# Spikes of a chunk in two batch rows instead of one block, mixed with the routing choices, and additions of returned rows in turns between two tiles

## The chip, the cores and the metric

The kernel runs on one core of a Trainium2 chip. The metric is the device time of one execution in microseconds (us). The engines of the core are TensorE (PE, with its weight loads as PEld), VectorE (DVE), ScalarE (ACT), GpSimd (POOL) and SyncE (SP), which here only issues DMAs. Each engine has its own queue and works through it in order; semaphores make one engine wait for another, or for its own earlier result.

## The reference, cut to what matters

The input `x` has 16 batch rows of 256 tokens with 256 channels; `cond` has one row of 256 channels for each batch row.

```python
# spikes: along the 256 tokens of a batch row
rates = relu(x) * 0.001
c = cond[:, None, :] + cumsum(rates, axis=1)
fl = floor(c)
prev = concatenate([floor(cond)[:, None, :], fl[:, :-1, :]], axis=1)
x = x + (fl - prev) / 0.001

# experts: 4096 tokens, 8 experts, 2 chosen for each token
shared = silu(xf @ w1) * (xf @ w3) @ w2
s = sigmoid(concatenate([xf, tf], -1) @ router_W)      # tf: cond of the token's batch row
topk_idx = top_k(s + router_bias, 2)
gates = s at the two, divided by their sum
routed = sum over the two chosen e of gate * (gelu(xf @ W1e[e]) @ W2e[e])
x = x + (shared + routed) / 3
```

## The kernel before

The 4096 tokens are cut into eight chunks of 512 tokens (two batch rows, `NB` = 2) and each chunk into four tiles of 128 tokens (`J` = 4). Channels lie on the partitions in two halves (`KD` = 2), so a chunk's spike data are 128 partitions by 2 x 2 x 256 elements.

**Spikes of one chunk** (`class Spikes`, driven by the generator `elementwise`). TensorE transposes the tokens (`turn`, L275), ScalarE writes `rates` (ReLU, L282) and a copy `xt` (L291). Then VectorE and ScalarE work on tags `tb`, `tot`, `base`, `ta`, `tc` of the pool `tmp`, one buffer each:
- `scan` (L306): a running sum in segments of 16 tokens, into `tb`; `keep` is zero at each segment's start.
- `sums` (L316, L320, L321): the segments' totals are copied shifted into `tot`, summed by a second scan into `base`, and added to every element, into `ta`.
- `start` and `whole` (ACT, L334, L343): `cond` is added as a bias, four times 256 elements, and the sum is cast to an integer in `tc`.
- `floor` (L358, L359): a compare and a subtract make the floor, in `tb` again, with the floor of `cond` in its first column (L348, VectorE).
- `spikes` (L370) and `add` (L378): the difference of neighbours, times 1000, plus `xt`, gives `x1`, for each batch row by itself.

From chunk 1 on, all but the last two take the whole chunk in one instruction of 1024 elements. Chunk 0 goes in three parts: two channel halves of its first batch row, then its second batch row.

**Routing of one chunk** (`route`). TensorE makes the logits `pl` (L426) from `x1`, VectorE clips them (`lt`, L435), TensorE turns them back (`pn`, L438), ScalarE takes the exponential (`ex`, L442), VectorE makes the sigmoid and picks the best expert twice (`first_best`, L452 to L458: maximum, compare, order, maximum, compare). These are instructions of 32 elements, each of which reads what the one before it wrote. `hot` (L470) marks both choices. From `hot` TensorE counts places (`pr`, L475 to L480) and turns `x1` into token rows (`px`, L496), which ScalarE copies into `x1t` (L497). VectorE makes the target rows `at_i` (L502 to L509), and GpSimd scatters the token rows to the buffer `xs` in device memory by indirect DMAs (L513).

**The shared expert** is a generator of work units (`unit`): `ph` matmuls (L536) of `x1` with `w1` and `w3`, silu on ScalarE (`as`, L546), a product on VectorE (`hs`, L547), `pa` matmuls (L563), and on VectorE `pa / 3` added to `x1t` (L574). A unit is spread by hand between the steps of `route` and `elementwise`: `next(ro)`, `next(el)`, `next(nxt)` and `unit()` stand in a written order in the main loop, where `el` is the chunk after the one that is routed. Between the start and the last chunk a scheduler may still change the order that results on each engine; at the start and from the last chunk on, the written order of PE, ACT and DVE is kept.

**Blocks and end.** After routing, SP loads up to 71 blocks of 128 rows; each goes through two expert products (L859, L881) and is scattered to `ys`. The last two shared chunks are left for the end, where they share time with `combine`: for each pair of token tiles (16 pairs) the returned rows `yc` are fetched from `ys`, and VectorE adds gate times row to `x1t`, twice for each tile, L996. Of the second choice's addition one input is the result of the first:

```python
            for j in range(2):
                last = x1ts[i][:, 2 * h + j, :, :FQ]
                for q in range(TOPK):
                    y = yc[:, j, TOPK - 1 - q]
                    nc.vector.scalar_tensor_tensor(
                        y, y, gates[:, q, t : t + 1], last, ALU.mult, ALU.add
                    )
                    last = y
```

The `pa` tiles lie in two PSUM buffers, and the `ph` tiles in three: a matmul into one of them waits until VectorE or ScalarE has read what was there.

Of the kernel before, what the change touches and what calls it, by code (L numbers as in the profile page):

```python
# [31 lines left out]
P = 128  # L32
N = 512
SEG = 16
# [4 lines left out]
def kernel(  # L39
# [203 lines left out]
    class Spikes:  # L243
# [3 lines left out]

        def __init__(self, i):  # L250
            def tile(tag, dt=F32, last=T, pool=tmp):
                return pool.tile([P, NB, KD, last], dt, tag=tag, name=f"{tag}_{i}")

            self.i, self.tile, self.xn = i, tile, xns.pop(i)
            self.xt = prep.tile([P, KD, N], F32, tag="xt", name=f"xt_{i}")
            self.rates = tile("rates")

        @staticmethod
        def cut(t, part):

            b, bb, k, kk = part
            if bb - b == 1:
                return t[:, b, k:kk, :].rearrange("p k t -> p (k t)")
            return t[:, b:bb, k:kk, :].rearrange("p b k t -> p (b k t)")

        def turn(self, part):

# [27 lines left out]
                xns[self.i + 2] = load_x(self.i + 2)  # L295

        def scan_tiles(self):
            self.seg = self.tile("tb")
            self.tot, self.base = self.tile("tot", last=NSEG), self.tile("base", last=NSEG)
            self.cs, self.ri = self.tile("ta"), self.tile("tc", I32)  # L300
            nc.vector.memset(self.tot[:, :, :, 0:1], 0.0)

        def scan(self, part):

            seg = self.cut(self.seg, part)
            nc.vector.tensor_tensor_scan(  # L306
                seg, keep[:, : seg.shape[1]], self.cut(self.rates, part), 0.0, ALU.mult, ALU.add
            )

        def sums(self, part):  # L310

            seg, tot, base, cs = (
                self.cut(t, part) for t in (self.seg, self.tot, self.base, self.cs)
            )
            n = tot.shape[1]
            nc.vector.tensor_copy(  # L316
                tot.rearrange("p (g s) -> p g s", s=NSEG)[:, :, 1:],
                seg.rearrange("p (g s q) -> p g s q", s=NSEG, q=SEG)[:, :, : NSEG - 1, SEG - 1],
            )
            nc.vector.tensor_tensor_scan(base, keep[:, :n], tot, 0.0, ALU.mult, ALU.add)  # L320
            nc.vector.tensor_tensor(  # L321
                cs.rearrange("p (s q) -> p s q", q=SEG),
                seg.rearrange("p (s q) -> p s q", q=SEG),
                base[:, :, None].to_broadcast([P, n, SEG]),
                ALU.add,
            )

        def start(self, part):
# [13 lines left out]

            nc.scalar.copy(self.cut(self.ri, part), self.cut(self.cs, part))  # L343

        def floor_tiles(self, pool=tmp, tag="tb", eng=nc.vector):

            self.fl = self.tile(tag, last=W, pool=pool)
            eng.tensor_copy(  # L348
                self.fl[:, :, :, 0].rearrange("p b k -> p k b"), cond_fl[:, :, ts(self.i, NB)]
            )  # L350
            self.x1 = x1s[self.i] = keepp.tile(
                [P, KD, N], F32, tag="x1", name=f"x1_{self.i}", bufs=6
            )

        def floor(self, part):

            up, ri = self.cut(self.cs, part), self.cut(self.ri, part)
            nc.vector.tensor_tensor(up, ri, up, ALU.is_gt)  # L358
            nc.vector.tensor_tensor(  # L359
                self.cut(self.fl, part).rearrange("p (g t) -> p g t", t=W)[:, :, 1:],  # L360
                ri.rearrange("p (g t) -> p g t", t=T),
                up.rearrange("p (g t) -> p g t", t=T),
                ALU.subtract,
            )

# [15 lines left out]

    def elementwise(i, sp=None):

        if sp is None:
            sp = Spikes(i)
            for k in range(KD):
                half = (0, NB, k, k + 1)
                pt = sp.turn(half)
                sp.rate(half, pt)
                sp.keep_x(half, pt)  # L390
            sp.next_load()
            yield
        part = (0, NB, 0, KD)
        sp.scan_tiles()
        sp.scan(part)
        yield
        sp.sums(part)
        yield
        sp.start(part)
        sp.whole(part)  # L400
        yield
        sp.floor_tiles()
        sp.floor(part)
        yield
        sp.spikes(part)
        yield
        sp.add(part)
        yield


# [2 lines left out]
    def route(i):  # L413
# [35 lines left out]
        def first_best(sc, q, key_at):  # L449
# [13 lines left out]
        nc.gpsimd.tensor_copy(  # L463
            x1t[:, :, :, FQ + 1], key_first[:, :, None].to_broadcast([P, J, NQ])
        )
        sel2 = small("sel2")
        nc.vector.scalar_tensor_tensor(sel2, hots[0], -BIG, sel, ALU.mult, ALU.add)
        hots.append(first_best(sel2, 1, small("second", (P, J))))
# [32 lines left out]
        row = small("row")  # L501
        nc.vector.tensor_tensor(row, pr, region, ALU.add)  # L502
        mine = small("mine", (P, TOPK, J, E))
        at = small("at", (P, TOPK, J))
        for q in range(TOPK):
            nc.vector.tensor_tensor(mine[:, q], row, hots[q], ALU.mult)
        nc.vector.tensor_reduce(at, mine, AX.X, ALU.add)
        at_i = small("at_i", (P, TOPK, J), I32)
        placed[i] = nc.vector.tensor_copy(at_i, at)  # L509
        yield  # L510
        for j in range(J):
            for q in range(TOPK):
# [101 lines left out]
    with tc.manual_schedule(engines={PE, ACT, DVE}):  # L614
        sp = Spikes(0)
        halves = [(0, 1, k, k + 1) for k in range(KD)]
        row = (1, 2, 0, KD)
        pts = [sp.turn(part) for part in halves]
        for part, pt in zip(halves, pts):
            sp.rate(part, pt)  # L620
        turn_cond()
        for part, pt in zip(halves, pts):
            sp.keep_x(part, pt)
        sp.scan_tiles()
        for part in halves:
            sp.scan(part)
            sp.sums(part)
            sp.start(part)
            sp.whole(part)
        cond_floor()  # L630
        sp.floor_tiles(pool=hid, tag="ht", eng=nc.gpsimd)
        pt = sp.turn(row)
        sp.rate(row, pt)
        sp.keep_x(row, pt)
        sp.next_load()
        for part in halves:
            sp.floor(part)
# [24 lines left out]
        unit(0.5)  # L662
# [7 lines left out]
    next(ro)  # L670
    next(el)
    next(ro)
    unit(0.5)
    next(ro)
    next(ro)
    next(ro)
    next(ro)
    next(el)
    unit(0.5)
    next(el)  # L680
    next(el)
    next(nxt)
    load_experts(0)
# [1 line left out]
    for i in range(2, NCHUNK):  # L685
        ro = route(i - 1)
        nxt = elementwise(i + 1) if i + 1 < NCHUNK else iter(())
        next(ro)
        next(el, None)
        unit()  # L690
        next(ro)
        next(el, None)
        next(ro)
        next(el, None)
        next(ro)
        unit()
        next(ro)
        next(el, None)
        next(ro)
        next(nxt, None)  # L700
        unit(1 + (i > 3 and i % 3 != 2) + (i == NCHUNK - 1))
        next(ro)
        next(el, None)
        next(ro)
        next(el, None)
        if i <= E // 2:
            load_experts(i - 1)
        el = nxt
# [3 lines left out]
    ro = route(NCHUNK - 1)  # L712
    next(ro)
    unit(0.5)
    next(ro)
    next(ro)
    next(ro)
# [268 lines left out]
    def combine():  # L986
        for n in range(SLOTS):
            fetch(n)
        for n, (i, h) in enumerate(pairs):
            yc = ycs.pop(n)  # L990
            for j in range(2):
                t = i * J + 2 * h + j
                last = x1ts[i][:, 2 * h + j, :, :FQ]
                for q in range(TOPK):
                    y = yc[:, j, TOPK - 1 - q]
                    nc.vector.scalar_tensor_tensor(  # L996
                        y, y, gates[:, q, t : t + 1], last, ALU.mult, ALU.add
                    )
# [56 lines left out]
```

## Time and profile before

| | us |
|---|---|
| median of 3 runs (336.89 to 337.3) | 337.07 |
| the profiled execution | 337.38 |
| its span, first to last instruction | 335.7 |
| busy: PE / DVE / POOL / ACT | 317.2 / 231.5 / 165.6 / 137.9 |

The profile is of one execution. The span is what its rows cover; some 1.7 us of that execution lie outside it. A row of the timeline has the start from the span's start, the busy time, the engine, the line of the kernel, the operation, the tile written and the tiles read, the shape, how many instructions were merged, and in brackets the idle time before it and what ended it. The granted clock of TensorE was 1.000 in the mean. A busy time runs to the end of the write, so on VectorE the next instruction can start before the last has ended.

### The profile page before, as it was taken

The page shows a single profiled execution, that of the slowest core. Times are in us where ns is not written, and L with a number is a line of the kernel's source. Part 1 is how long each engine was busy: PE and PEld are TensorE (multiplying, and loading weights), DVE is VectorE, ACT ScalarE, POOL GpSimd, SP SyncE. Part 2 cuts the span into 40 slices and gives each one's busy share as a digit, 9 for nine tenths or more (in the row PEclk, how much of TensorE's full clock was granted, in tenths as well). Part 3 has the DMA queues.
Part 4 walks back from the last instruction along what each step waited for, and adds up shares of the span by engine and source line. Part 5 has one row for each costly group of instructions (what it writes and reads, how often), then busy time and mean ns, then how long its engine had stood idle before and what let it go on. Part 6 is the DMA issues. An engine that isn't in the chain of part 4 may idle for free. (4 is left out here: it accounts for less than half of the span.)

```text
span 335.7 us, 6544 instructions
## 1 busy us (share of the span) xinstructions
PE 317.2 (94%) x1674; PEld 233.9 (70%) x1674; DVE 231.5 (69%) x656; ACT 137.9 (41%) x287; POOL 165.6 (49%) x197
## 2 busy tenths in 40 slices
PE   3799998999989999999999999999999999999985
PEld 2587644547546745746699998999999998474574
DVE  4677979999999996652467655555546551299993
ACT  4547385644675372040244443444444434201100
POOL 7000274787478687662045555555555565123220
PEclk9999999999999999999999999999999999999999
DMA  6999533242222112354456665765666662499913
GB/s 174 255 217 215 146 114 98 88 136 100 79 81 99 65 64 86 109 194 102 73 109 149 155 149 142 165 140 126 156 150 151 157 146 80 164 364 408 397 70 125
DMA packets 62534, 50.34 MB, mean 150 GB/s; under 512 B 42607, under 2 KB 52864, under 8 KB 62497
## 3 DMA queue, kind: packets, MB, share of 16 engines
q1 hardware_dynamic: 42240, 26.19, 32.0%
q0 software_dynamic: 7456, 20.86, 17.0%
q10 hardware_dynamic: 12800, 2.88, 5.0%
q8 instruction: 14, 0.23, 0.3%
q14 instruction: 24, 0.19, 0.2%
HBM read 27.44 MB, written 22.84 MB: 150 GB/s over the span
## 5 line engine op out<-in xcount | busy, mean ns | idle before, releaser
L536 PE MATMUL ph<-x,w_sb 128*128 128x512 f32 (+1 forms) x288 | 119.3, 561 | 4.9 <-DVE x L378 4.2
L890 POOL DMA_INDIRECT ys<-yb,to x67 | 66.2, 988 | 67.0 <-ACT yb L889 56.4
L513 POOL DMA_INDIRECT xs<-x1t,at_i x64 | 78.8, 1232 | 38.8 <-ACT xt L291 18.7
L536 PEld LDWEIGHTS ph<-x,w_sb 128*128 128x128 f32 x288 | 54.2, 196 | 53.5 <-issue 42.0
L859 PEld LDWEIGHTS phe<-xbt,w1e 128*128 128x128 f32 x536 | 70.3, 191 | 4.7 <-ACT hbt L867 0.9
L859 PE MATMUL phe<-xbt,w1e 128*128 128x128 f32 x536 | 70.7, 275 | 0.7 <-DVE xbt L832 0.7
L881 PE MATMUL py<-we,hbt 128*128 x268 | 68.9, 380 | 0.2 <-ACT hbt L867 0.2
L827 DVE COPY w1e<-we 128x512 f32 x67 | 29.1, 435 | 45.3 <-PE phe L859 43.8
L563 PE MATMUL pa<-w_sb,hs 128*128 128x256 f32 x256 | 58.2, 381 | 1.4 <-DVE x1t L574 1.1
L563 PEld LDWEIGHTS pa<-w_sb,hs 128*128 128x128 f32 x256 | 48.0, 190 | 11.1 <-issue 2.8
L881 PEld LDWEIGHTS py<-we,hbt 128*128 128x128 f32 x268 | 45.9, 191 | 3.9 <-ACT hbt L867 0.4
L546 ACT ACTIVATE as<-ph 128x512 f32<-128x512 f32 (+1 forms) x36 | 19.9, 553 | 64.5 <-PE ph L536 51.8
L867 ACT ACTIVATE hbt<-phe 128x256 f32<-128x256 f32 x67 | 25.8, 384 | 45.6 <-PE phe L859 35.2
L547 DVE TENSOR_TENSOR hs<-as,ph 128x512 f32<-128x512 f32 (+1 forms) x36 | 22.4, 623 | 27.5 <-PE ph L536 20.8
L889 ACT COPY yb<-py 128x256 f32<-128x256 f32 x67 | 24.9, 372 | 22.7 <-PE py L881 22.2
L832 DVE STREAM_TRANSPOSE xbt<-xb 128x256 f32<-128x256 f32 x67 | 29.3, 437 | 0.0
L306 DVE TENSOR_TENSOR_SCAN tb<-keep,rates 128x1024 f32<-128x1024 f32 (+2 forms) x10 | 18.8, 1876 | 1.4 <-ACT rates L282 1.3
L497 ACT COPY x1t<-px 128x512 f32<-128x512 f32 x16 | 8.6, 592 | 25.1 <-PE px L496 25.1
L589 POOL DMA_DIRECT2D out_dram<-yc x8 | 5.8, 729 | 23.9 <-DVE yc L996 22.1
L334 ACT ACTIVATE ta<-ta,cond_t 128x256 f32<-128x256 f32 x32 | 14.1, 498 | 8.1 <-DVE ta L321 7.1
L463 POOL COPY x1t<-first 128x16 f32<-128x16 f32 x8 | 4.2, 519 | 23.1 <-DVE first L456 23.1
L574 DVE SCALAR_TENSOR_TENSOR x1t<-pa,x1t 128x512 f32<-128x512 f32 x14 | 9.6, 684 | 6.3 <-PE pa L563 6.3
(135 smaller groups left out, 268.2 us busy)
## 6 DMA issues: line engine op xcount, KB each, us to landing
xb<-xs SPq DMA_DIRECT2D x184, 33.0 KB
yc<-ys SPq DMA_DIRECT2D x8, 512.0 KB
we<-ys SPq DMA_DIRECT2D x8, 512.0 KB
xn<-in_x_dram SPq DMA_DIRECT2D x7, 512.0 KB
xb<-xs ACTq DMA_DIRECT2D x84, 33.0 KB
we<-in_L_cond_W1e_dram SPq DMA_DIRECT2D x8, 256.0 KB
we<-in_L_cond_W2e_dram SPq DMA_DIRECT2D x8, 256.0 KB
out_dram<-yc POOLq DMA_DIRECT2D x8, 256.0 KB, 4.3
```

What stands on the lines that cost most here:

```text
L513: nc.gpsimd.indirect_dma_start(out=xs_w[(i * J + j) * TOPK + q][:, :], out_offset=bass.IndirectOffsetOnAxis(ap=at_i[:, q, j : j + 1], axis=0),
L536: nc.tensor.matmul(ph, lhsT=w[:, k, ts(u, P)], rhs=x1[:, k, cols], start=(k == 0), stop=(k == KD - 1),)
L546: nc.scalar.activation(act, ps[0], AF.Silu)
L547: nc.vector.tensor_tensor(ht[:, u, cols], act, ps[1], ALU.mult)
L563: nc.tensor.matmul(pa[:, q, :], lhsT=ht[:, s, ts(n * h + q, P)], rhs=w2_sb[:, s, :], start=(s == 0), stop=(s == KS - 1),)
L827: nc.vector.tensor_copy(w, we[:, bass.ds(off, KD * HE)])
L832: nc.vector.transpose(xt.rearrange("p g k r -> p g (k r)"), block[b].pop("xb")[:, :, :FQ])
L859: nc.tensor.matmul(ph[:, m, :].rearrange("p (g r) -> p g r", r=Q), lhsT=w[:, k, ts(m, P)], rhs=xt[:, :, k, :], start=(k == 0), stop=(k == ...
L867: nc.scalar.activation(ht, ph, AF.Gelu)
L881: nc.tensor.matmul(py, lhsT=ht[:, k, :], rhs=we[:, bass.ds(off + KD * HE + k * D, D)], start=(k == 0), stop=(k == KH - 1),)
L889: nc.scalar.copy(yb, py)
L890: nc.gpsimd.indirect_dma_start(out=ys_w[b][:, :], out_offset=bass.IndirectOffsetOnAxis(ap=to[:, b : b + 1], axis=0), in_=yb, in_offset=Non ...
```

## The change

Four things are done. A chunk's spikes go through `scan`, `sums`, `start`, `whole`, `floor`, `spikes` and `add` in two parts, one for each batch row (`one`, `two`); the parts are mixed in the written order. The running sums are made in place: the scan writes `tb`, the second scan reads the segments' last elements directly, and its sums are added to all segments but the first of a row, in `tb` again; the floor goes to `ta`, its first column is copied by ScalarE (for chunk 0 by GpSimd). In `route` a `yield` is put between the first and the second choice, so that work of `elementwise` can stand there, and the place `at_i` is reduced straight into integers. In `combine` the two tiles of a pair take turns: the first choice of both, then the second choice of both.

```diff
         def scan_tiles(self):
-            self.seg = self.tile("tb")
-            self.tot, self.base = self.tile("tot", last=NSEG), self.tile("base", last=NSEG)
-            self.cs, self.ri = self.tile("ta"), self.tile("tc", I32)
-            nc.vector.memset(self.tot[:, :, :, 0:1], 0.0)
+            self.cs = self.tile("tb")
+            self.upto, self.ri = self.tile("tot", last=NSEG), self.tile("tc", I32)
...
         def sums(self, part):
-            n = tot.shape[1]
-            nc.vector.tensor_copy(
-                tot.rearrange("p (g s) -> p g s", s=NSEG)[:, :, 1:],
-                seg.rearrange("p (g s q) -> p g s q", s=NSEG, q=SEG)[:, :, : NSEG - 1, SEG - 1],
-            )
-            nc.vector.tensor_tensor_scan(base, keep[:, :n], tot, 0.0, ALU.mult, ALU.add)
+            upto = self.cut(self.upto, part)
+            n = upto.shape[1]
+            cs = self.cut(self.cs, part).rearrange("p (s q) -> p s q", q=SEG)
+            nc.vector.tensor_tensor_scan(
+                upto, keep[:, :n], cs[:, :, SEG - 1], 0.0, ALU.mult, ALU.add
+            )
+            cs = cs.rearrange("p (g s) q -> p g s q", s=NSEG)[:, :, 1:]
+            upto = upto.rearrange("p (g s) -> p g s", s=NSEG)[:, :, : NSEG - 1, None]
             nc.vector.tensor_tensor(
-                cs.rearrange("p (s q) -> p s q", q=SEG),
-                seg.rearrange("p (s q) -> p s q", q=SEG),
-                base[:, :, None].to_broadcast([P, n, SEG]),
-                ALU.add,
+                cs, cs, upto.to_broadcast([P, n // NSEG, NSEG - 1, SEG]), ALU.add
             )
...
-        def floor_tiles(self, pool=tmp, tag="tb", eng=nc.vector):
-            self.fl = self.tile(tag, last=W, pool=pool)
-            eng.tensor_copy(
-                self.fl[:, :, :, 0].rearrange("p b k -> p k b"), cond_fl[:, :, ts(self.i, NB)]
-            )
+        def floor_tiles(self, copy=nc.scalar.copy):
+            self.fl = self.tile("ta", last=W)
+            copy(self.fl[:, :, :, 0].rearrange("p b k -> p k b"), cond_fl[:, :, ts(self.i, NB)])
...
     def elementwise(i, sp=None):
+        one, two = [(b, b + 1, 0, KD) for b in range(NB)]
         if sp is None:
             sp = Spikes(i)
-            for k in range(KD):
-                half = (0, NB, k, k + 1)
-                pt = sp.turn(half)
-                sp.rate(half, pt)
-                sp.keep_x(half, pt)
+            for part in (one, two):
+                pt = sp.turn(part)
+                sp.rate(part, pt)
+                sp.keep_x(part, pt)
             sp.next_load()
             yield
-        part = (0, NB, 0, KD)
         sp.scan_tiles()
-        sp.scan(part)
-        yield
-        sp.sums(part)
-        yield
-        sp.start(part)
-        sp.whole(part)
-        yield
-        sp.floor_tiles()
-        sp.floor(part)
-        yield
-        sp.spikes(part)
-        yield
-        sp.add(part)
+        sp.scan(one)
+        yield
+        sp.sums(one)
+        sp.start(one)
+        sp.whole(one)
+        sp.scan(two)
+        yield
+        sp.sums(two)
+        sp.start(two)
+        sp.whole(two)
+        sp.floor_tiles()
+        yield
+        sp.floor(one)
+        yield
+        sp.spikes(one)
+        sp.add(one)
+        sp.floor(two)
+        yield
+        sp.spikes(two)
+        sp.add(two)
         yield
...
         nc.gpsimd.tensor_copy(
             x1t[:, :, :, FQ + 1], key_first[:, :, None].to_broadcast([P, J, NQ])
         )
+        yield
         sel2 = small("sel2")
...
-        at = small("at", (P, TOPK, J))
-        nc.vector.tensor_reduce(at, mine, AX.X, ALU.add)
         at_i = small("at_i", (P, TOPK, J), I32)
-        placed[i] = nc.vector.tensor_copy(at_i, at)
+        with nc.allow_low_precision(reason="one whole number and zeros are added"):
+            placed[i] = nc.vector.tensor_reduce(at_i, mine, AX.X, ALU.add)
...
-        sp.floor_tiles(pool=hid, tag="ht", eng=nc.gpsimd)
+        sp.floor_tiles(copy=nc.gpsimd.tensor_copy)
...
     next(ro)
     next(el)
     next(ro)
+    next(el)
+    next(ro)
     unit(0.5)
     next(ro)
-    next(ro)
-    next(ro)
-    next(ro)
     next(el)
+    next(ro)
+    next(ro)
+    next(ro)
     unit(0.5)
-    next(el)
     next(el)
     next(nxt)
...
         next(ro)
         next(el, None)
         next(ro)
+        next(el, None)
+        next(ro)
         unit()
         next(ro)
         next(el, None)
...
         unit(1 + (i > 3 and i % 3 != 2) + (i == NCHUNK - 1))
         next(ro)
-        next(el, None)
         next(ro)
         next(el, None)
...
-            for j in range(2):
-                t = i * J + 2 * h + j
-                last = x1ts[i][:, 2 * h + j, :, :FQ]
-                for q in range(TOPK):
+            last = [x1ts[i][:, 2 * h + j, :, :FQ] for j in range(2)]
+            for q in range(TOPK):
+                for j in range(2):
+                    t = i * J + 2 * h + j
                     y = yc[:, j, TOPK - 1 - q]
                     nc.vector.scalar_tensor_tensor(
-                        y, y, gates[:, q, t : t + 1], last, ALU.mult, ALU.add
+                        y, y, gates[:, q, t : t + 1], last[j], ALU.mult, ALU.add
                     )
-                    last = y
+                    last[j] = y
```

More of the change, by code (lines that the diff above doesn't have):

```diff
@@ L250, in __init__, with tile @@
         def __init__(self, i):
-            def tile(tag, dt=F32, last=T, pool=tmp):
-                return pool.tile([P, NB, KD, last], dt, tag=tag, name=f"{tag}_{i}")
+            def tile(tag, dt=F32, last=T):
+                return tmp.tile([P, NB, KD, last], dt, tag=tag, name=f"{tag}_{i}")
             self.i, self.tile, self.xn = i, tile, xns.pop(i)
@@ L259, in cut @@
         def cut(t, part):
[L261 to L264, printed above, removed]
+            b, _, k, kk = part
+            return t[:, b, k:kk, :].rearrange("p k t -> p (k t)")
         def turn(self, part):
@@ L297, in scan_tiles @@
         def scan_tiles(self):
-            self.seg = self.tile("tb")
-            self.tot, self.base = self.tile("tot", last=NSEG), self.tile("base", last=NSEG)
-            self.cs, self.ri = self.tile("ta"), self.tile("tc", I32)
-            nc.vector.memset(self.tot[:, :, :, 0:1], 0.0)
+            self.cs = self.tile("tb")
+            self.upto, self.ri = self.tile("tot", last=NSEG), self.tile("tc", I32)
         def scan(self, part):
-            seg = self.cut(self.seg, part)
+            cs = self.cut(self.cs, part)
             nc.vector.tensor_tensor_scan(
-                seg, keep[:, : seg.shape[1]], self.cut(self.rates, part), 0.0, ALU.mult, ALU.add
+                cs, keep[:, : cs.shape[1]], self.cut(self.rates, part), 0.0, ALU.mult, ALU.add
             )
         def sums(self, part):
-            seg, tot, base, cs = (
-                self.cut(t, part) for t in (self.seg, self.tot, self.base, self.cs)
-            )
-            n = tot.shape[1]
-            nc.vector.tensor_copy(
-                tot.rearrange("p (g s) -> p g s", s=NSEG)[:, :, 1:],
-                seg.rearrange("p (g s q) -> p g s q", s=NSEG, q=SEG)[:, :, : NSEG - 1, SEG - 1],
-            )
-            nc.vector.tensor_tensor_scan(base, keep[:, :n], tot, 0.0, ALU.mult, ALU.add)
+            upto = self.cut(self.upto, part)
[3 more added lines that the diff above has]
+                upto, keep[:, :n], cs[:, :, SEG - 1], 0.0, ALU.mult, ALU.add
+            )
+            cs = cs.rearrange("p (g s) q -> p g s q", s=NSEG)[:, :, 1:]
+            upto = upto.rearrange("p (g s) -> p g s", s=NSEG)[:, :, : NSEG - 1, None]
             nc.vector.tensor_tensor(
-                cs.rearrange("p (s q) -> p s q", q=SEG),
-                seg.rearrange("p (s q) -> p s q", q=SEG),
-                base[:, :, None].to_broadcast([P, n, SEG]),
-                ALU.add,
+                cs, cs, upto.to_broadcast([P, n // NSEG, NSEG - 1, SEG]), ALU.add
             )
@@ L359, in floor @@
             nc.vector.tensor_tensor(
-                self.cut(self.fl, part).rearrange("p (g t) -> p g t", t=W)[:, :, 1:],
-                ri.rearrange("p (g t) -> p g t", t=T),
-                up.rearrange("p (g t) -> p g t", t=T),
+                self.cut(self.fl, part).rearrange("p (k t) -> p k t", t=W)[:, :, 1:],
+                ri.rearrange("p (k t) -> p k t", t=T),
+                up.rearrange("p (k t) -> p k t", t=T),
                 ALU.subtract,
@@ L672 @@
     next(ro)
+    next(el)
+    next(ro)
     unit(0.5)
+    next(ro)
+    next(el)
     next(ro)
@@ L676 @@
     next(ro)
-    next(ro)
-    next(el)
     unit(0.5)
-    next(el)
     next(el)
```

## The prediction, made before the changed kernel was run

> **What bounds the kernel now.** I read the page first.
>
> ```profile
> PE 317.2 (94%) x1674; PEld 233.9 (70%) x1674; DVE 231.5 (69%) x656; ACT 137.9 (41%) x287; POOL 165.6 (49%) x197
> PE   3799998999989999999999999999999999999985
> DVE  4677979999999996652467655555546551299993
> ```
>
> TensorE is the bound over the whole span. VectorE is full in two stretches only, slices 5 to 15 (routing, to about 125 us) and the end from 293 us. The change lies in both. So I cut the first at the matmul `pr` (L475), which waits for `hot`, and asked for the busy time from each `pr` to the next.
>
> ```profile
> 35.13:52.36 17.23, 16.28 (x72) 8.54 (x72) 14.77 (x39) 10.22 (x17) 10.56 (x9) 1.00 0.36 122
> 52.36:65.73 13.37, 13.16 (x62) 6.63 (x62) 12.86 (x39) 9.17 (x17) 7.89 (x6) 1.00 0.29 93
> 65.73:84.22 18.49, 18.05 (x90) 11.63 (x89) 17.92 (x43) 9.15 (x16) 14.64 (x13) 1.00 0.34 117
> 84.22:94.99 10.77, 10.14 (x55) 5.36 (x55) 10.32 (x35) 8.23 (x15) 5.91 (x4) 1.00 0.28 86
> 94.99:113.21 18.22, 17.34 (x86) 11.24 (x86) 17.72 (x43) 8.34 (x15) 14.85 (x13) 1.00 0.23 83
> 113.21:123.98 10.77, 10.22 (x54) 5.35 (x55) 10.36 (x34) 8.23 (x15) 7.17 (x6) 1.00 0.18 64
> ```
>
> Columns: stretch, length, then busy PE, PEld, DVE, ACT, POOL. Both PE and DVE are nearly full. Matmul starts lie 0.429 us apart (128x512), 0.216 (128x256) and 0.109 (transposes); by these the six stretches hold 15.8, 12.4, 17.6, 9.8, 16.7 and 9.8 us of matmuls, 82.1 in 88.85. TensorE loses 6.8 us, and DVE sets the pace. Two timelines give the rest.
>
> ```profile
> 112.97 0.19 DVE L470 TENSOR_TENSOR hot<-chosen,chosen 128x32 bf16<-128x32 f32 x1
> 113.07 0.69 DVE L370 TENSOR_TENSOR x<-tb 128x512 f32<-128x512 f32 x1
> 114.98 0.62 ACT L282 ACTIVATE rates<-pt 128x512 f32<-128x512 f32 x1
> 116.61 2.29 DVE L306 TENSOR_TENSOR_SCAN tb<-keep,rates 128x1024 f32<-128x1024 f32 x1
> 117.67 1.28 ACT L546 ACT_TABLE_LOAD   x1
> 118.97 0.60 ACT L546 ACTIVATE as<-ph 128x512 f32<-128x512 f32 x1
> ```
> ```profile
> 300.13 0.47 DVE L996 SCALAR_TENSOR_TENSOR yc<-yc,gates,x1t 128x256 f32<-128x256 f32 x1
> 300.64 0.48 DVE L996 SCALAR_TENSOR_TENSOR yc<-yc,gates 128x256 f32<-128x256 f32 x1
> 301.04 0.48 DVE L996 SCALAR_TENSOR_TENSOR yc<-yc,gates,x1t 128x256 f32<-128x256 f32 x1
> 326.45 1.99 PE L563 MATMUL pa<-w_sb,hs 128*128 128x256 f32 x8 [1.15 <-DVE x1t L574]
> 328.74 3.72 PE L563 MATMUL pa<-w_sb,hs 128*128 128x256 f32 x16 [0.30 <-DVE we L574]
> ```
>
> First: the rates of the next chunk end 2.63 us after `hot` starts (`pr`, `px`, `pt` on PE, two copies and the ReLU on ACT lie between), and DVE has 3.6 us of adds to do before its scan needs them. Second: an addition that reads what the one before it wrote starts 0.51 us after it, an independent one 0.40. All DVE rows obey this: next start at the end plus 0.034 if dependent, minus 0.084 if not, so a dependent step costs 0.118 more.
>
> **The start.** Each half of chunk 0 loses the copy L316 (steps of 0.21) and adds 240 instead of 256 elements. The second half's add, the floors behind it and `x1` come 0.44 us earlier, and so the first L536 matmuls, which waited 3.75 and 0.50 us. From 11.9 to 15.7 us those matmuls step at 0.427, half rate; if that phase doesn't move with them, half the gain is lost. I take 0.35. The changed instruction list lets chunk 1's scan pass the second row's add of chunk 0, but TensorE has two more `pa` matmuls (0.43) before it needs that row. Chunk 1 is finished before `hot` of chunk 0, with 1.7 us of chunk 1's matmuls put ahead of `pr`. By DVE steps `hot` comes at 36.1 and `pr` at 36.5; before, `pr` was at 35.13 with 1.7 less done. Gain **0.35**.
>
> **The routing stretch, DVE.** Per chunk in steps, before: scan 2.20, copy 0.12, base scan 0.20, add 1.14, memset and floor column 0.13, compare and subtract 2.27, spikes and adds 2.40: 8.46. After: two scans 2.27 (1.217 each), two sum scans 0.28 (0.225, the 32-element row; with a strided read the change alone has it, between 0.19, the 16-element row, and 0.29, the 64-element one: 0.1 a chunk either way; the strided copy of 60 at 0.203 says that stride costs nothing, so 0.225), two adds 1.15, compares and subtracts 2.42, spikes and adds 2.40: 8.52. The split costs nothing net. `at_i` loses a cast (0.08 in steps; the reduce into int32 is known from L851, 0.170). In-place output is free (L358 in place 1.219, L321 not 1.224). The floor column goes to ACT, which is 41% busy: 0.19 a chunk, beside DVE. The gain is in mixing: with 512-element instructions between the choices, dependent steps fall from 22 to 14 in two chunks. All DVE steps from one `hot` to the second next: 28.7 before (traced: 28.99), 27.8 after. DVE saves 0.45 a chunk.
>
> **The routing stretch, what is late next.** In the new order the adds of chunk i+1 stand before `hot` of chunk i; after `hot` only one add and the places remain, and DVE reaches the scan of chunk i+2 1.5 us after `hot` started. The rates are ready at 2.63. So the scan waits 1.1 us, and the choices, hidden products and PSUM evictions behind it in DVE's queue wait too; then TensorE at the next `pr`. `hot` to `hot` is 2.66 plus the steps from scan to `hot`:
> - stretch 1: 12.8, plus 1.2 because ACT takes both rows' order as bias, table load, exp, and exp ends 5.8 after the scan where DVE wants it at 4.6: 16.7; matmuls 15.4
> - 2: 12.4, so 15.05; matmuls 13.7
> - 3, 4, 5: 12.3, so 14.9 each; matmuls 13.7, 14.1, 13.7
> - 6: 10.3, so 12.95; matmuls 10.65
>
> Together 89.4, matmuls 81.2, TensorE loses 8.2 instead of 6.8: **1.4 lost**. After that the queues are the same and TensorE bound (DVE idle 1.4 and 1.8 us there). POOL's scatters follow `at_i` and the ACT copies as before; the last set starts after `at_i` of the last chunk and is waited for by SP's block loads, with DVE's `hs` later than them (1.63 us wait on PE), so 0.2 less there is hidden. SP's queue is unchanged.
>
> **ACT.** The list has four more table loads, since every chunk now alternates exp and silu. In stretches 2 to 6 exp should end 3.0 us after the scan (second `xt` copy 1.45, load 1.28, exp 0.2) and DVE wants it at 4.6. Trace: the load takes 1.28 and the next ACTIVATE starts 0.02 later. The Trainium skill, "ScalarE: Activation LUTs", What ACT_TABLE_LOAD costs, adds a drain of about 1.38 us (2.66 in all): then exp ends at 4.4, still in time, but stretch 1 would lose 1.4 more. The trace decides: 1.28.
>
> **The end.** Each pair of row tiles has four additions, two of them dependent: 1.83 us by starts. In turns: 4 x 0.40 = 1.60. Sixteen pairs: 3.7 us of DVE. The chain of waits is DVE from 292.7 to 328.7, but TensorE stands only 1.15 + 0.30 us, 1.77 against its steps. With 2.8 us saved by the last `hs` (ready 316.7, run at 319.01), DVE waits for PE instead; `x1t` L574 of chunk 6 runs at 324.0, before its bank is wanted at 325.2. TensorE gains all: **1.75**. The Trainium skill, "VectorE: DVE Perf Modes", The DRAIN you can't avoid, speaks against it: a wait between chained operations costs nothing extra and the next cannot start before the pipe is empty. By that rule the end gives 0 and the whole is +1.05, 338.1. The rows show 0.51 against 0.40, so I keep 1.75.
>
> **Sum.** -0.35 + 1.4 - 1.75 = -0.7 on the profiled 337.38 (span 335.7): 336.7; the median shown, 337.07, lies 0.31 under that execution, so **336.4**.
>
> **Rivals.**
> - *The rates are in time* (20%). For: TensorE has 1 us free in every stretch and could be early. Against: it waits at `pr` in order, and 2.63 was met at every chunk. If the wait were gone, DVE's 13.8 would meet TensorE's 13.7 and some 0.5 us a stretch would be lost, 3 in all: -0.35 - 3.8 - 1.75, 331.2; half of it, 334.
> - *ACT answers late, slower* (15%). ACT queues the second row's first bias before the cast of the first row. Add 0.66, wait 0.10, bias 0.415, cast 0.61, about 1.83 us after the second add starts, and DVE wants it at 1.95. Any slip over 0.12 is a new DVE stall in each chunk; at 0.5 in five of them 338.9.
> - *Turns bring nothing* (7%): 338.1, as above.
>
> My forecast has 58%, 335.4 to 337.4 by itself: 0.1 to 0.15 of error in six loops, 0.2 at the start. Faster or slower counts beyond 0.2% (0.67 us), about what a measurement of this kernel can tell from no change: the line at 336.4 halves the forecast a little in favour of faster (34 to 24). Faster 0.34 + 0.20 = 0.54; same 0.24 + 0.02; slower 0.15 + 0.05. The range leaves out the lower half of the first rival and the upper half of the second: 333.5 to 338.7.
>
> **What would show it.** Right: DVE's scan waits about 1.1 us for ACT rates in most chunks; TensorE's wait for `hot` about doubles; at the end additions start 0.40 apart, PE's two waits at L563 vanish and DVE waits for `ph` and `pa`. Wrong: no scan wait and `pr` to `pr` near 14 (faster), a DVE wait for `tc` at the compare (slower), or additions still 0.51 apart.

## The result and the profile after

The changed kernel takes 336.39 us (median of 22 runs, 335.4 to 336.94) against 337.12 us before (22 runs, 336.01 to 338.1): a ratio of 0.9976, interval 0.9966 to 0.9985. A second set of runs gave 336.29 against 337.31: 0.997, interval 0.9957 to 0.9983. It is faster by 0.7 to 1.0 us; both intervals exclude no change, though not by much. Ratios here and below are of runs within 1.5% of the fastest of their kernel; runs outside that, 17 of 35 of the kernel before, came in the first set of the experiments alone. The profiled execution of after took 336.61 us with a span of 334.9, and so lies 0.2 above its median.

The page of after: shares of engines, VectorE's tenths in 40 slices, and the chain of waits by engine and by line.

```profile
PE 315.8 (94%) x1674; PEld 233.6 (70%) x1674; DVE 225.6 (67%) x658; ACT 145.4 (43%) x305; POOL 152.9 (46%) x197
...
DVE  4678789989899995661277755565545553089993
...
PE 13%; DVE 0%; issue 0%
PE ph L533 7%; PE pa L560 6%; DVE we L571 0%
```

Before, the chain that ended last was 10% VectorE (the additions of returned rows). Now it is TensorE alone (13%): the end is bound by matmuls. VectorE has 5.9 us less to do, and TensorE is as full as before.

The same stretches as before, from each `pr` (now L473) to the next: length, then busy PE, PEld, DVE, ACT, POOL.

```profile
36.96:53.62 16.66, 15.54 (x69) 7.79 (x67) 13.64 (x39) 10.84 (x20) 8.76 (x9) 1.00 0.39 132
53.62:68.77 15.15, 14.06 (x70) 7.82 (x69) 14.69 (x41) 10.49 (x19) 9.95 (x9) 1.00 0.32 103
68.77:83.66 14.89, 13.94 (x76) 9.32 (x76) 13.61 (x40) 9.36 (x17) 9.06 (x9) 1.00 0.32 114
83.66:98.61 14.95, 14.60 (x68) 7.73 (x69) 13.69 (x40) 10.53 (x20) 8.49 (x9) 1.00 0.34 107
98.61:113.55 14.94, 13.98 (x80) 9.72 (x79) 13.81 (x40) 9.44 (x18) 9.49 (x9) 1.00 0.20 74
113.55:126.51 12.96, 11.17 (x57) 5.44 (x57) 12.07 (x37) 9.73 (x18) 8.16 (x7) 1.00 0.18 63
```

The prediction had 16.7, 15.05, 14.9, 14.9, 14.9 and 12.95. VectorE is no longer full (13.6 of 14.9), and TensorE isn't either: in such a loop both wait for something else. VectorE's timeline, its rows from one `hot` to the next scan, shows what.

```profile
83.42 0.18 DVE L468 TENSOR_TENSOR hot<-chosen,chosen 128x32 bf16<-128x32 f32 x1
83.54 0.69 DVE L369 SCALAR_TENSOR_TENSOR x<-x,xt 128x512 f32<-128x512 f32 x1
...
84.81 0.22 DVE L506 TENSOR_REDUCE at_i<-mine 128x8 int32<-128x64 f32 x1
86.08 1.23 DVE L303 TENSOR_TENSOR_SCAN tb<-keep,rates 128x512 f32<-128x512 f32 x1 [1.06 <-ACT rates L281]
```

One add is left behind `hot`, VectorE reaches the scan 1.6 us after `hot` began, and the rates come at 2.66: a wait of 1.06 us. It stands in five of the six stretches (1.32, 1.07, 1.06, 0.78, 0.47). In stretch 2 two operations of the shared expert fill the gap, and the scan starts 2.71 us after `hot` all the same. The kernel before has no such wait: of its groups of instructions, the seven scans of whole chunks, with the idle time of VectorE before them last.

```profile
L306 DVE TENSOR_TENSOR_SCAN tb<-keep,rates 128x1024 f32<-128x1024 f32 x7 | 16.0, 2285 | 0.0
```

The end. VectorE's timeline first: the additions now stand in rows of two, 0.87 us for two, a new row every 0.79. Then TensorE's timeline to its last matmul.

```profile
319.23 0.87 DVE L997 SCALAR_TENSOR_TENSOR yc<-yc,gates,x1t 128x256 f32<-128x256 f32 x2
320.02 0.87 DVE L997 SCALAR_TENSOR_TENSOR yc<-yc,gates 128x256 f32<-128x256 f32 x2
```
```profile
297.05 7.07 PE L560 MATMUL pa<-w_sb,hs 128*128 128x256 f32 x32
303.95 13.90 PE L533 MATMUL ph<-x,w_sb 128*128 128x512 f32 x32
317.69 13.98 PE L560 MATMUL pa<-w_sb,hs 128*128 128x256 f32 x64
```

Neither `pa` wait of before is left. From the first late `pa` to the last matmul's end is 34.62 us; it was 36.59.

Where the 0.80 us of span went (335.67 to 334.87), by the points that both traces share:

| part | before | after | difference |
|---|---|---|---|
| to `pr` of chunk 0, with 1.72 us for four 128x512 matmuls that after has put ahead of it | 35.13 + 1.72 | 36.96 | +0.11 |
| from there to the first expert matmul, same matmuls | 130.25 - 1.72 | 130.09 | +1.56 |
| experts, to the first late `pa` | 130.49 | 130.00 | -0.49 |
| late `pa` to the last | 36.59 | 34.62 | -1.97 |

### The profile page after: what moved, and what is told of

The parts are those of the page before. It is cut to its first block, busy times and chain, and to the rows that moved or that the text cites. A ratio compares the mean times of both kernels' runs of the same rounds, so it can differ in the third digit from the quotient of the medians.

```text
span 334.9 us, 6557 instructions
## 1 busy us (share of the span) xinstructions
PE 315.8 (94%) x1674; PEld 233.6 (70%) x1674; DVE 225.6 (67%) x658; ACT 145.4 (43%) x305; POOL 152.9 (46%) x197
## 5 line engine op out<-in xcount | busy, mean ns | idle before, releaser
L510 POOL DMA_INDIRECT xs<-x1t,at_i x64 | 68.9, 1077 | 49.2 <-issue 16.8
L303 DVE TENSOR_TENSOR_SCAN tb<-keep,rates 128x512 f32<-128x512 f32 (+1 forms) x17 | 19.6, 1153 | 8.0 <-ACT rates L281 7.8
L327 ACT ACTIVATE tb<-tb,cond_t 128x256 f32<-128x256 f32 x32 | 14.9, 502 | 6.5 <-DVE tb L317 6.5
L460 POOL COPY x1t<-first 128x16 f32<-128x16 f32 x8 | 2.2, 277 | 26.4 <-DVE first L453 26.4
```

The source lines that it names most:

```text
L510: nc.gpsimd.indirect_dma_start(out=xs_w[(i * J + j) * TOPK + q][:, :], out_offset=bass.IndirectOffsetOnAxis(ap=at_i[:, q, j : j + 1], axis=0),
```

## The experiments

Times of a set are read against the kernel before in that set. In the first set the kernel before scattered from 339.2 to 349.4 us (35 runs), so its ratios decide little and its traces are read instead. That set holds `e1`, `e2`, `e3` and the first run of `e7`; why it scattered is open. Several of these kernels move matmuls from one stretch to another, so I compare the time from `pr` of chunk 0 to the first expert matmul, which holds the same matmuls in all that are built on the changed kernel: 130.09 us in after, 130.10 in its second profile.

**Turns alone** (`e1_turns_only`): the kernel before with

```
-            for j in range(2):
...
-                for q in range(TOPK):
+            last = [x1ts[i][:, 2 * h + j, :, :FQ] for j in range(2)]
+            for q in range(TOPK):
+                for j in range(2):
```

> The kernel before with one part of the change: the additions of returned rows taken in turns. Theory (a dependent VectorE step starts 0.118 us later than an independent one): the additions start 0.40 apart, TensorE's waits of 1.15 and 0.30 us at pa near the end go, 1.75 us less by the prediction, up to 1.97 by what the changed kernel showed: ratio to before 0.994 to 0.995. Rival (a dependent step costs nothing of its own): additions still 0.51 apart in a pair, ratio 1.000.

Measured: ratio 1.0003, interval 0.9967 to 1.004. By the time alone the turns bring nothing: the interval holds the 1.000 of the rival and not the 0.994 to 0.995 of the theory. The trace says otherwise; TensorE's timeline at the end of this kernel:

```profile
299.83 7.07 PE L563 MATMUL pa<-w_sb,hs 128*128 128x256 f32 x32
306.74 13.90 PE L536 MATMUL ph<-x,w_sb 128*128 128x512 f32 x32
320.47 13.98 PE L563 MATMUL pa<-w_sb,hs 128*128 128x256 f32 x64
```

The end takes 34.62 us, to the hundredth what it takes in after, 1.97 less than in before. This execution lost its time elsewhere: from `pr` of chunk 0 to the experts it takes 134.12 us against 130.25, and 2.2 us of that lie in the third stretch, where nothing was edited. So by the trace the turns are worth 1.97 us at the end; that the time of this set does not show it stays open, and `e11` below tests it where the runs agree.

**Spikes and choices alone** (`e2_spikes_only`): the changed kernel with the additions in the old order.

> The changed kernel with the additions in the old order, so the two-row spikes, the in-place sums and the choices between them are left by themselves. Theory: the routing stretch and the start together cost 1.05 us by the prediction and 1.2 by subtracting 1.97 from the measured -0.73: ratio to before 1.003 to 1.004. Rival (this part is what gained, and the turns are nothing): ratio 0.998 or lower.

Measured: ratio 0.9969, interval 0.9937 to 1.0001. That is a miss for the theory (1.003 to 1.004): by the time the part gains. But the set's scatter is larger than the disputed microsecond, and the experts, which the edit does not touch, take 135.35 us in the profiled execution against 130.00 in after, so I don't take it as decided. In the trace the end is that of before, with its waits (TensorE's timeline):

```profile
322.75 8.80 PE L560 MATMUL pa<-w_sb,hs 128*128 128x256 f32 x40
332.68 1.99 PE L560 MATMUL pa<-w_sb,hs 128*128 128x256 f32 x8 [1.14 <-DVE x1t L571]
334.98 3.72 PE L560 MATMUL pa<-w_sb,hs 128*128 128x256 f32 x16 [0.30 <-DVE we L571]
```

It takes 36.59 us, and the routing stretches are those of after but for the third (16.66, 15.13, then 15.36 instead of 14.89, 14.96, 14.95, 12.97). So in the traces the two parts don't touch each other, and the lost time of the routing belongs to this one. That it costs about a microsecond in the whole can be estimated from the sets that agree: `e11`, with the same end of 34.62 us and the old spikes, lies 2.07 us under before, the changed kernel 0.7 to 1.0, so the rest of the change costs some 1.0 to 1.3 us.

**Additions without the dependence** (`e11_no_dependence`): the kernel before, order unchanged, with

```
                     nc.vector.scalar_tensor_tensor(
                         y, y, gates[:, q, t : t + 1], last, ALU.mult, ALU.add
                     )
-                    last = y
```

> The kernel before, additions in its own order, but the second addition of a row reads the copied row and not what the first wrote; the first choice's part is left out of the sum so. Theory (it is the dependence that costs 0.118 us): additions 0.40 apart, 34.6 us from the first late pa to the last as with the turns, ratio to before 0.994 to 0.995. Rival (it is the order of the tiles, not the dependence): still 0.51 after the first of a row, 36.6 us, ratio 1.000.

Measured: 335.35 us against 337.42, ratio 0.9924, interval 0.99 to 0.9949. VectorE's timeline of it at the end:

```profile
300.07 1.66 DVE L996 SCALAR_TENSOR_TENSOR yc<-yc,gates,x1t 128x256 f32<-128x256 f32 x4
301.65 1.67 DVE L996 SCALAR_TENSOR_TENSOR we<-we,gates,x1t 128x256 f32<-128x256 f32 x4
```

Four additions in a step of 1.58, 0.40 each, in the old order, and an end of 34.62 us. Here the time agrees as well: 2.07 us less, of which the end gives 1.97. It is the dependence that costs, not the order of the tiles; the turns only put an independent addition between two dependent ones.

**VectorE's work kept behind `hot`** (`e7_work_behind_hot`, then `e7_again` beside the changed kernel): from chunk 2 on, the last subtract, the spikes and the add of the second row are queued behind `hot` of the chunk before.

```
...
-        sp.spikes(two)
-        sp.add(two)
+        with tc.issue_after(hot_of[i].ins) if i > 1 else nullcontext():
+            if i > 1:
+                sp.less(two, *sp.rest)
+            sp.spikes(two)
+            sp.add(two)
...
```

> The changed kernel with the last subtract, the spikes and the add of the second row held behind hot in VectorE's queue, the rates where they were. It attacks the same wait from the other side: 1.2 us of VectorE's work fills the time in which it waited for the rates. Theory: no scan wait, three more dependent steps in the second choice (0.35), so hot to hot 14.9 - 1.1 + 0.35 = 14.15 in stretches 2 to 5 and less in 6; some 3.5 us less than the changed kernel, 333, ratio to before 0.987 to 0.989. Rival (TensorE needs the second row right behind hot, so what hot gains is lost at pl): pr to pr unchanged, 336 to 337, ratio 0.997 to 1.000.

> Last subtract, spikes and add of the second row behind hot, once more, beside the changed kernel. In the first run pr to pr was 15.8, 13.9, 14.1, 13.9, 15.7, 15.8, 14.8. Theory: stretches 2 to 4 again near 14; if TensorE's waits of stretches 5 and 6 were of that run alone, 14 and 12.5 there, 333 to 334, 0.991 to 0.994 of the changed kernel. Rival (stretches 5 to 7 pay back what 1 to 4 gain): 335.5 to 336.4, 0.997 to 1.000 of it.

> The changed kernel itself, once more, beside the others of this set so that they can be compared with it on the same chip. Theory: ratio to before 0.9976 as measured; pr to pr 16.7, 15.1, 14.9, 14.9, 14.9, 13.0; 34.6 us from the first late pa to the last. What is open is the start: pr of chunk 0 at 36.96 in the one execution seen, 36.5 by the prediction.

Measured: the first time 335.73 us, ratio 0.9814 in the scattered set, not used. The second time 334.34 against 337.31, ratio 0.9908, interval 0.9877 to 0.9939, where the changed kernel in the same set had 336.29 (0.997, 0.9957 to 0.9983). Its timeline from `hot` to the scan, VectorE's rows, its windows from `pr` to `pr`, and the scan's waits from 36 to 142 us in after and then here:

```profile
66.21 0.19 DVE L477 TENSOR_TENSOR hot<-chosen,chosen 128x32 bf16<-128x32 f32 x1
66.31 0.68 DVE L356 TENSOR_TENSOR ta<-tc,tb 128x512 f32<-128x512 int32 x1
...
67.23 0.68 DVE L367 TENSOR_TENSOR x<-ta 128x512 f32<-128x512 f32 x1
...
69.37 1.22 DVE L303 TENSOR_TENSOR_SCAN tb<-keep,rates 128x512 f32<-128x512 f32 x1
```
```profile
66.45:80.58 14.13, 13.59 (x71) 8.41 (x71) 13.82 (x40) 9.70 (x18) 9.34 (x10) 1.00 0.33 114
80.58:94.51 13.93, 13.59 (x70) 8.38 (x71) 13.65 (x40) 9.84 (x18) 9.18 (x10) 1.00 0.34 112
94.51:110.14 15.63, 14.88 (x77) 9.54 (x77) 14.29 (x41) 9.81 (x18) 10.35 (x11) 1.00 0.23 84
110.14:125.94 15.80, 14.97 (x70) 8.41 (x71) 14.44 (x41) 10.30 (x19) 9.03 (x9) 1.00 0.19 69
```
```profile
DVE tb L303 <- ACT rates L281: 4.7, 5, 1.3
```
```profile
DVE tb L303 <- ACT rates L281: 1.3, 1, 1.3
```

From chunk 2 on, where the edit acts, the scan no longer waits, and where TensorE is busy for 13.59 us the stretch lasts 13.93 or 14.13. The long ones, 15.63 and 15.80, hold more work of TensorE, 14.9 us busy, and the last stretch (14.84 instead of 16.57) holds less. From `pr` of chunk 0 to the experts it is 127.94 us, 2.16 less than the changed kernel beside it, and the time fell by 1.95. So the wait for the rates paced this stretch, and the work that the two rows had moved ahead of `hot` was the cover that it had lost. My expected 3.5 us was too much: it gave every stretch what VectorE's chain saves, but a stretch of 13.93 with 13.59 us of TensorE in it has little left to win, and VectorE's waits for exp grew from 3.0 to 5.1 us.

**Rates earlier** (`e3_rates_early`, `e8_rates_before_px`): the other side of the same wait. In the first the transposes and rates of the next chunk are issued ahead of `pr`, in the second between `pr` and `px`. The edit of the second:

```
         next(ro)
         next(el, None)
-        next(ro)
         next(nxt, None)
+        next(ro)
```

> The changed kernel with the transposes and rates of the next chunk issued ahead of pr and px instead of behind px. Theory (VectorE, held at the scan for the rates, paces the stretch): the scan's waits of 0.8 to 1.1 us go, pr to pr falls from 14.9 to 13.8 in stretches 2 to 5, TensorE's own work being 13.7; 4 to 5.5 us less than the changed kernel in all, some 331 to 332.4, ratio to before 0.982 to 0.986. Rival (the wait only moves, to exp, to the activations behind the table loads or to the hidden products): pr to pr stays above 14.5, 335 to 336.4, ratio 0.994 to 0.998.

> The changed kernel with the next chunk's transposes and rates between pr and px, a smaller move than ahead of pr: 1.07 us earlier on TensorE and 1.08 on ACT. Theory (the scan's wait for the rates paces the stretch): that wait goes, pr to pr 13.8 to 14.0 in stretches 2 to 5, some 4 us less than the changed kernel, 332 to 333. Rival (VectorE's list shifts with it: the scan goes ahead of lt and the biases ahead of exp on ACT, so exp comes late and the choices wait): pr to pr of 15 or more, 336 to 345, as the larger move was slower (355).

Measured: the larger move 355.28 us, ratio 1.0375 in the scattered set, interval 1.0315 to 1.0434: a miss for both expectations. There VectorE's list had taken the next chunk's scan and sums in among the choices, `pr` to `pr` was 19.2 and 17.1 in the first two stretches, and TensorE once stood 9.0 us before `pn` for `lt`. What `lt` itself waited for the profile does not name; that cause stays open. TensorE also lost its full clock: the granted clock was 0.975 or 0.976 in each of its six runs, and this is the fifth stretch of the profiled one, with 0.93 in the third column from the end:

```profile
98.67:122.86 24.19, 17.87 (x85) 11.61 (x84) 17.14 (x46) 10.46 (x19) 11.81 (x14) 0.93 0.19 68
```

In the trace the granted clock is 0.50 in three pieces (106.6 to 110.0, 123.7 to 127.1, 144.1 to 154.3), 17.0 us in all, in which TensorE is busy for 10.8. A step of 128x256 takes 0.427 us at half rate and 0.216 at full, so about half of that, some 5 us, is what the lower clock costs (an estimate). The smaller move: 335.26 against 337.31, ratio 0.9931, interval 0.9907 to 0.9954, 1.03 us less than the changed kernel beside it. To the experts it takes 128.68 us, 1.4 less. The forecast of 13.8 to 14.0 from `pr` to `pr` did not come: stretches 2 to 5 are 15.3 to 15.9, some of it because they hold more matmuls. VectorE's rows of one:

```profile
70.75 1.23 DVE L303 TENSOR_TENSOR_SCAN tb<-keep,rates 128x512 f32<-128x512 f32 x1 [0.34 <-ACT rates L281]
...
77.81 0.18 DVE L441 TENSOR_SCALAR ex<-ex 128x32 f32<-128x32 f32 x1
...
84.55 0.18 DVE L468 TENSOR_TENSOR hot<-chosen,chosen 128x32 bf16<-128x32 f32 x1
```

The wait fell from 1.07 to 0.34 here as meant (4.7 to 2.2 over all), but exp's result is taken up only 7.06 us after the scan (4.5 in after, 71.19 to 75.66), because ACT does biases and a cast ahead of its table load, and the choices then stand with little between them. Each theory had half of it: the wait was worth something, and the list shifted.

**Both moves** (`e9_both_moves`): `e7` and `e8` together.

> Work behind hot (e7) and the rates ahead of px (e8) together. Theory (both took away the same wait): they do not add; between 333.5 and 335, not below 333.3. Rival (they took away different waits): the gains of 1.95 and 1.03 us against the changed kernel add to 333.3 or less, ratio to before 0.988 or lower.

Measured: 335.11 against 337.42, ratio 0.9924, interval 0.99 to 0.9948. They don't add, as the theory said, though 335.11 lies just above its range; 129.51 us to the experts is even more than `e7` alone has. In the trace the scan waits as little as in `e7` (1.3 us, once), while VectorE waits 6.3 us for exp (5.1 in `e7`) and TensorE 2.8 us at `pn` for `lt`. So the second move found no wait for rates left to take away, and its shift of the lists remained.

**A linear function in the hidden product** (`e5_linear_hidden`):

```
-                nc.scalar.activation(act, ps[0], AF.Silu)
+                nc.scalar.activation(act, ps[0], AF.Identity)
```

> The changed kernel with a linear function in place of silu in the shared hidden product: the product's value is left out, and with it the alternation of exp and silu on ACT, so no table loads up to the experts. Theory: a load is 1.28 us of ACT that lies beside other work in stretches 2 to 5 (pr to pr stays 14.9, held by the rates); the exp wait of 1.2 us in stretch 1 goes, and TensorE's waits for late activations (1.12, 1.31 and 0.35 us) go: 1.5 to 3 us less than the changed kernel. Rival (the loads drain the engine and delay every chunk's rates and biases): pr to pr falls by 0.5 or more in stretches 2 to 5 too, 5 us or more less.

Measured: 333.91 against 337.31, ratio 0.9901, interval 0.9863 to 0.9939, 2.4 us less than the changed kernel in the set and 1.9 less to the experts. VectorE's waits from 36 to 142 us:

```profile
DVE tb L303 <- ACT rates L281: 5.8, 6, 1.3
...
DVE ex L441 <- ACT ex L439: 1.8, 1, 1.8
```

The waits for rates stay (4.7 us in five in after), exp's fall from 3.0 to 1.8, and TensorE's 2.4 us of waits for late activations are gone; its waits for `hot` rise from 2.4 to 3.7. So the alternation of exp and silu costs about 2 us here through a few waits, and it isn't what holds the scan.

**exp ahead of the biases** (`e12_exp_first`), on top of `e7`:

```
         sp.sums(one)
-        sp.start(one)
+        with tc.issue_after(ex_of[i].ins) if i > 1 else nullcontext():
+            sp.start(one)
...
         next(ro)
+        next(ro)
         next(el, None)
-        next(ro)
         next(el, None)
```

The second cut is of the main loop: exp of a chunk has to be written ahead of the biases that are queued behind it.

> Work behind hot (e7) and, on top of it, exp of a chunk issued on ACT ahead of the next chunk's biases. In e7 VectorE waited for exp 1.2 to 1.8 us in four stretches, 5.1 in all, and ACT took the biases first while it had been idle 1.9 us. Theory (the loop is paced by VectorE's chain through exp, once the rates are out of it): those waits go or fall under 0.5, 1 to 2.5 us less than e7, 331.8 to 333.3, ratio to before 0.984 to 0.988. Rival (TensorE has no idle left to win: each stretch keeps about 1 us at small matmuls and hand-overs, or the biases come late for the compare instead): 334 to 335, ratio 0.990 to 0.993.

Measured: 333.78 against 337.42, ratio 0.9889, interval 0.9865 to 0.9913. Its first two stretches and VectorE's wait for exp over all:

```profile
35.67:49.13 13.46, 12.43 (x63) 6.72 (x62) 11.53 (x35) 10.27 (x18) 8.96 (x9) 1.00 0.57 179
49.13:64.28 15.15, 15.03 (x71) 8.27 (x71) 14.87 (x42) 10.65 (x19) 9.15 (x9) 1.00 0.31 103
```
```profile
DVE ex L451 <- ACT ex L449: 3.3, 2, 1.8
```

VectorE's waits for exp fall from 5.1 us in `e7` to 3.3, both of them behind 106 us. To the experts it is 127.43 us, 0.5 less than `e7`: less than the 1 that the theory asked for, and 333.78 lies between the two expectations. It has the lowest time of those that compute the whole and beats both kernels; that it beats `e7` rests on the trace, since the two intervals overlap.

**The kernel before, a second profile** (`b0_before_again`):

> The kernel before once more, for a second profile of it. Open: whether its first matmul at 3.66 us, its full TensorE rate from 15.9 us, and one expert block of 2.25 us among 65 of 1.76 belong to the kernel or to the one execution seen. If to the execution: pr of chunk 0 at 35.1 plus what the first matmul is later, no block above 1.9, and the span 335.2 to 335.7.

Measured: 336.87 us, span 335.2. No expert block takes more than 1.88 us, the first matmul starts at 3.93, `pr` of chunk 0 at 35.19, and the end takes 36.60. The half microsecond in the experts belonged to the one execution.

## Why the prediction was right, and where its steps were off

- *The direction and the size.* 336.4 was forecast and 336.39 came. The sum of its parts was -0.7, and the profiled difference -0.80 of span. That the two times agree to 0.01 us is luck: against the profiled pair the terms are off by +0.46 (start), +0.16 (routing), -0.22 (end) and -0.49 (experts, which have no term), and these nearly cancel. That the turns win more than the routing loses was forecast for the right reason.
- *The routing stretch, +1.4.* Right. By the prediction's own count TensorE loses 89.55 - 81.2 = 8.35 us in the six stretches (8.2 forecast, 6.8 before). All six lengths were met within 0.1, the exp wait of stretch 1 came at 1.20 us (forecast 1.2), and the scan's waits at 0.8 to 1.1 in stretches 3 to 5. Stretch 2, where the scan finds work ahead of it and does not wait, has its forecast length too, since the scan starts no earlier. `e7` shows that it was that wait: with work put into it, 2.16 us come back.
- *"TensorE's wait for `hot` about doubles."* Wrong. The listed wait fell from 2.9 to 2.4 us, because other hand-overs take part of the time: `ph` for late activations (2.4 us in two) and `pn` (1.3 us in five). The sum of the idle time was right, the label on it was not.
- *The start, -0.35.* Off by size. In the profiled pair it is +0.11, and +0.10 in the second profiles of both kernels. The first `ph` did start earlier, as forecast; the rows of TensorE's timeline of before, then after:

```profile
10.21 1.22 PE L536 MATMUL ph<-x,w_sb 128*128 128x256 f32 x2 [3.75 <-DVE x L378]
11.93 7.08 PE L536 MATMUL ph<-x,w_sb 128*128 128x256 f32 x22 [0.50 <-DVE x L378]
```
```profile
9.89 1.22 PE L533 MATMUL ph<-x,w_sb 128*128 128x256 f32 x2 [3.12 <-DVE x L369]
11.61 7.55 PE L533 MATMUL ph<-x,w_sb 128*128 128x256 f32 x22 [0.49 <-DVE x L369]
```

  It is 0.32 earlier, though the first matmul began 0.32 later (3.98 against 3.66; in the second profile of before it began at 3.93 and the first `ph` at 10.30, 0.46 more between them than here). But the next 22 took 0.47 longer, since the full rate came later in that execution. The prediction named this doubt and put half the gain on it; here it took the whole. In `e1` and `e2`, where these 22 took 6.51 and 6.43, `pr` of chunk 0 came at 34.61 and 35.78: with the 1.72 us of matmuls, 0.55 gained. A loss that I had not listed is the 0.35 us that `ph` waits at 32.12 for an activation behind a table load.
- *The end, -1.75.* Right in mechanism, small by 0.22. The term was the time that TensorE stood against its steps, given as 1.77; by the starts of the rows in the prediction the two stands are 1.30 and 0.56 us, 1.86. The whole stretch gives more still: the last 64 `pa` took 15.95 us before (316.51 to 332.46) and take 13.98 now without a stand, 1.97 less. What the turns save beyond TensorE's stands is lost, as forecast: VectorE waits for `pa` three times at the very end.
- *The experts, 0.* An expert block of 2.25 us instead of 1.76 in the profiled execution of before gave after 0.49 that is none of its doing. The sum was set against that execution; the 0.31 by which the median lay under it took up most of that.
- *The rivals.* The rates were not in time (five waits). ACT was not late at the compare in the loop; the one `tc` wait there is (1.12 us at 28.10) lies in the start. (The four times that the prediction adds for it make 1.79, not 1.83.) The turns do bring what they should. The Trainium skill ("VectorE: DVE Perf Modes", The DRAIN you can't avoid) has eight copies that took as long with a semaphore after each as with one at the end; here `e11` measures 0.40 without the dependence where before has 0.51 with it, so here the dependence has a price. The prediction took from the section only that the next operation waits for an empty pipe; the section also says that one which is not held starts earlier, and additions that start 0.40 us apart while each takes 0.48 do start so.

## What to carry to other kernels

Mixing short dependent steps with long independent ones saves the 0.118 us of each dependence, but it pulls the long ones ahead of the short chain's result; what they covered behind it lies open then. Ask of each instruction that a better order moves forward which wait it was hiding. And compare stretches that hold the same matmuls: a stretch that got longer may only have been given more to do.

## What the hardware showed that I had not expected

The moment at which TensorE goes over from half to full rate (steps of 0.427 and 0.216 us for 128x256) moves between executions of the same start: the same 22 matmuls took 7.08 and 7.05 us in two profiles of before and 6.51 in `e1`, whose start is the same; 7.55 and 7.58 in two of after and 6.43 in `e2`, whose start is that of after. That is up to 1.15 us of spread between starts that are the same in the kernel, more than the change as a whole. It also goes with the set of runs: in the four profiles of the first set the 22 took 6.40 to 6.51 us, in the four of the second 7.56 to 7.72, and in the four of the third, where the start of before gave both 7.05 and 6.51, 6.34 to 7.05. What sets the moment no run here shows. A gain ahead of it can't be read from one pair of profiles.
